# A gated cross-attention and ternary feed-forward block on one core: 16-bit tiles turned on TensorE in place of the DMA, one ring of eight PSUM banks, and new orders

## The chip, the core and the metric

The kernel runs on one core of one Trainium2 chip. The core has a matrix engine (TensorE, PE in the profile, with its weight loads shown apart as PEld), VectorE (DVE), ScalarE (ACT), GpSimd (POOL), and SyncE (SP), which here only issues DMAs. On-chip data lie in SBUF, 128 partitions wide; TensorE's results go to PSUM, which is used here as eight banks of 128 x 512 32-bit numbers. The metric is the device time of one execution in microseconds.

## The reference, cut to what matters

The input is 8 sequences of 512 tokens with 512 features, and for each sequence 64 context tokens. A first half adds a scaled cross-attention, a second half a scaled feed-forward block:

```python
def bit_linear(x, w, b):
    gamma_x = jnp.clip(jnp.max(jnp.abs(x), axis=-1, keepdims=True), 1e-05, None)
    scale_x = 127.0 / gamma_x
    x_dq = jnp.clip(jnp.round(x * scale_x), -128.0, 127.0) / scale_x
    ...
    gamma_w = jnp.clip(jnp.mean(jnp.abs(w)), 1e-05, None)
    w_dq = jnp.clip(jnp.round(w / gamma_w), -1.0, 1.0) * gamma_w
    ...
    return jnp.einsum('bsd,hd->bsh', x_ste, w_ste) + b
gate = jax.nn.silu(bit_linear(x, gate_w, gate_b))
val = bit_linear(x, val_w, val_b)
return bit_linear(gate * val, out_w, out_b)
...
x = x + jnp.tanh(g_xattn[0]) * _L0_xattn_ref(_layernorm(x, axis=-1), ctx_2048, mask_BxS2_ik0, ...)
x = x + jnp.tanh(g_ffn[0]) * _L0_ffn_ref(_layernorm(x, axis=-1), L0_ffn_gate_w, ...)
```

The attention has 16 heads of 32 features, masked softmax over the 64 context tokens, an output projection and a layernorm of its result. In the feed-forward block the activations are rounded to whole numbers from -128 to 127 per token and the weights to -1, 0 or 1; the hidden width is 2,048.

## The kernel before

A batch is one sequence, four token tiles of 128. Everything runs once, with the batches in a software pipeline: while the feed-forward tiles of batch b-1 are worked off, the attention of batch b and the layernorm of batch b+1 go on beside them. The stages that the change and the prediction touch are these, with their lines in the kernel before.

Layernorm and queries. Statistics come from VectorE and GpSimd (`ln1_stats`). For batches 0 and 1 the normalised tiles are turned by 32-bit transposes on TensorE (`ln1_turn`, L293). For the later ones the transposed input is loaded from memory (`load_turned`); the four means and four reciprocal deviations of each token are written to memory and read back spread over all partitions (`ln1_rows`, L228 and L230), so that a row of them holds, for each token in turn, eight numbers. VectorE subtracts the mean rows (L253), reading every eighth number, and GpSimd multiplies in two halves (L262). Queries are 4 x 4 32-bit matmuls (L304).

Attention. Scores (L340) of one half of the heads fill four banks, ScalarE takes the exponential (L353), TensorE sums (L367) and weighs the values (L415). The reciprocal sums travel over memory in four small DMAs (`rows`, `dense`, `over`, `R`). The projection (L442) is 4 x 4 32-bit matmuls for each token tile.

Feed-forward. For a token tile: `ffn_in` rounds on ScalarE and VectorE to whole numbers in 16 bits (`xq`), and a DMA transpose on SP's queue turns them (`xqT`, L687). `ffn_mid` fills four banks in each of two halves: four bias matmuls of 32 rows (L700), then 16 matmuls with the ternary gate and value weights (L705). `ffn_gate` takes silu on ScalarE (L715) and the product on VectorE (L716). `ffn_quant` finds the largest magnitude over 2,048 numbers (L734), `ffn_quant2` rounds a half on ScalarE (L752) and VectorE (L753) and again a DMA transpose turns it (`hqT`, L758). `ffn_out` is 16 matmuls (L766), `ffn_end` adds and stores. The scales of four tiles' tokens are turned by one DMA transpose for each batch (`uT`, L676).

PSUM. One pool of four banks (`bank`) serves all but the feed-forward's fours, which have a pool of four of their own (`psum4`, `four`). In the closing part every other four takes its banks from the first pool.

Order. `beginning`, `opening`, `attend_third`, `attend`, `attend_last` and `closing_flat` are lists written out by hand, one call after the other; `tile_in`, `tile_mid` and the like take the next token tile in their own sequence. `in_order` fixes each engine to the order in which its instructions were issued. So an instruction that waits holds up all behind it on its engine, and a DMA that waits holds up all behind it on SP's queue.

A second path, `general_path`, is there for inputs outside a common range. It isn't run with these inputs.

Of the kernel before, what the change touches and what calls it, by code (L numbers as in the profile page):

```python
# [9 lines left out]
F32 = mybir.dt.float32  # L10
# [7 lines left out]
P = 128  # L18
# [9 lines left out]
def common_path(  # L28
# [67 lines left out]
    psum = ctx.enter_context(tc.tile_pool(name="psum", bufs=4, space=bass.MemoryType.PSUM))  # L96
    psum4 = ctx.enter_context(tc.tile_pool(name="psum4", bufs=4, space=bass.MemoryType.PSUM))
# [5 lines left out]

    def bcast(vec, dst):
        nc.sync.dma_start(out=dst, in_=vec.partition_broadcast(P))

    ident = const.tile([P, P], F32, name="ident")
    make_identity(nc, ident)
    ones = const.tile([P, P], F32, name="ones")
    nc.gpsimd.memset(ones, 1.0)  # L110

    idle = psum4.tile([P, NW], F32, tag="four", name="idle")
# [110 lines left out]
    def ln1_rows(b):  # L223

        if b >= B:
            return
        rows = dram.tile([P, 2 * ST], F32, tag="lnrows", name="lnrows")
        nc.sync.dma_start(out=rows, in_=st_[b, "ln1"][1].rearrange("p r t -> p (r t)"))  # L228
        row = work.tile([P, P * 2 * ST], F32, tag="hs", name="row")
        nc.sync.dma_start(  # L230
            out=row, in_=rows.rearrange("p k -> (p k)").partition_broadcast(P)
        )
        row = row.rearrange("q (p r t) -> q r t p", r=2, t=ST)
        for i in range(2):
            st_[b, "row", i] = row[:, i].unsqueeze(1)
# [11 lines left out]
    def ln1_turned(b):  # L247

        if b >= B:
            return  # L250
        hT = st_[b, "hT"].rearrange("q c (t p) -> q c t p", t=ST)
        m = st_[b, "row", 0].to_broadcast([P, DC, ST, P])
        nc.vector.tensor_tensor(hT, hT, m, ALU.subtract)  # L253

    def ln1_turned_end(b):
        if b >= B:
            return
        hT = st_[b, "hT"].rearrange("q c (t p) -> q c t p", t=ST)
        r = st_[b, "row", 1].to_broadcast([P, DC // 2, ST, P])
        for h in range(2):  # L260
            half = hT[:, h * DC // 2 : (h + 1) * DC // 2]
            nc.gpsimd.tensor_tensor(half, half, r, ALU.mult)  # L262
# [250 lines left out]
    def ternary_load(name, *parts):  # L513

        w, chunks = {"gate": (gate_w, DC), "val": (val_w, DC), "out": (out_w, FC)}[name]
        if name not in st_:
            acc = [
                stage.tile([P, 1], F32, tag=f"acc{q}", name="acc", bufs=2) for q in range(DC)
            ]
            half = stage.tile([P, 3], F32, tag="half", name="half", bufs=2)  # L520
            st_[name] = {}, half, acc
# [9 lines left out]
    def magnitude(name, q, vector=False):  # L531
        part, _, acc = st_[name]
        if vector:
            nc.vector.tensor_reduce(
                acc[q], part[q], AX.X, ALU.add, apply_absolute_value=True
# [4 lines left out]
            junk, part[q], AF.Abs, accum_out=acc[q], saturate=False  # L540
        )

    def mean(i, name):
# [3 lines left out]
        for q in range(DC):  # L547
            nc.tensor.matmul(ps[:, 0:1], ones, acc[q], start=(q == 0), stop=(q == DC - 1))
        g = gw[:, i : i + 1]
        nc.vector.tensor_scalar(g, ps[:, 0:1], 1.0 / (F * D), 1e-5, ALU.mult, ALU.max)  # L550
# [71 lines left out]
    def ffn_stats(b, step):  # L622
# [47 lines left out]
        for r in range(4):  # L670
# [3 lines left out]
            )  # L674
        uT = fp.tile([P, ST, P], BF16, tag="uT", name="uT", bufs=2)
        nc.sync.dma_start_transpose(out=uT, in_=u.rearrange("p g k -> p (g k)"))  # L676
        st_[b, "in"] = rstd, sgv, uT

    def ffn_in(b, i):
# [4 lines left out]
        xq = fp.tile([P, D], BF16, tag="xq", name="xq", bufs=2)  # L684
        nc.vector.tensor_scalar(xq, h2, MAGIC, None, ALU.subtract)
        xqT = fp.tile([P, DC, P], BF16, tag="xqT", name="xqT", bufs=2)
        nc.sync.dma_start_transpose(out=xqT, in_=xq)  # L687
        st_[b, "xqT", i] = xqT
        st_[b, "h", i] = None

    def ffn_mid(b, i, jj, pool=psum4, tag="four"):


        xqT, uT = st_[b, "xqT", i], st_[b, "in"][2]
# [52 lines left out]
    def ffn_quant2(b, i, half):  # L747
        h, s = st_[b, "h", i], st_[b, "h_s", i]
        for half in (half,):
            cols = slice(half * F // 2, (half + 1) * F // 2)  # L750
            hq = fp.tile([P, F // 2], BF16, tag="hq", name="hq", bufs=2)
            nc.scalar.activation(h[:, cols], h[:, cols], AF.Identity, scale=s, bias=magic)  # L752
            nc.vector.tensor_scalar(hq, h[:, cols], MAGIC, None, ALU.subtract)  # L753

            late = b * ST + i - (B - 2) * ST
            pool, tag, bufs = (fp, "hqT", 2) if late < 0 else (xpool, f"x{late // 2 % 2}", ST)
            hqT = pool.tile([P, FC // 2, P], BF16, tag=tag, name="hqT", bufs=bufs)
            nc.sync.dma_start_transpose(out=hqT, in_=hq)  # L758
            st_[b, "hqT", i, half] = hqT
# [74 lines left out]
    def beginning():  # L834

        ternary_load("gate", 2)
        ternary_load("gate", 0)
        ternary_load("gate", 1)
        ternary_load("gate", 3)
        load_queries()  # L840
        load_x(ST, ST + 1)
        constants()
        ln1_stats(0, 0, 1)
        load_rows()
        later_rows()
        keys(0)
        keys(1)
        ternary_load("val", 0)
        keys(2)
        ln1_stats(0, 2, 3)  # L850
        keys(3)
        keys_end(0)
        ln1(0, 1)
        load_x(ST + 2, ST + 3)
        keys_end(1)
        context_values(0)
        ln1(0, 0)
        keys_end(2)
        keys_end(3)
        ln1_turn(0, 0)  # L860
        ln1_turn(0, 1)
        ln1(0, 2)
        context_values_end(0)
        ln1(0, 3)
        magnitude("gate", 0, True)
# [1161 lines left out]
```

## Time and profile before

The median of three runs is 724.24 us (722.26 to 726.79).

| | us |
|---|---|
| median of the runs | 724.24 |
| profiled execution, its own time | 719.48 |
| its span, first to last instruction | 717.6 |
| TensorE busy in it | 687.8 |
| VectorE busy | 559.0 |
| ScalarE busy | 361.5 |
| GpSimd busy | 175.5 |
| a steady batch (from 345.3 to 428.3) | 83.0 |

A row of a group gives the line of the kernel, engine and operation, output<-inputs, sizes and count; after the first bar the busy time of the group and the mean of one in ns; after the second the idle time of the engine just ahead of them, and what ended it. Bars of matmuls overlap, so the busy time of a group is less than count times mean. 32-bit matmuls of 512 columns leave two records each. A row of waits gives who waited for whom, the total in us, how often, and the longest. In the timeline the first number is the start, the second the length.

The other rows that matter for the change: the 64 DMA transposes of `hq` land 3.2 us after their issue and the 32 of `xq` 2.4 us after; the matmuls of 512 columns on 16-bit tiles have bars of 380 ns; a ScalarE copy of 128 x 512 out of PSUM (L377) takes 589 ns and a cast of 128 x 1024 (L615) 1,050 ns; the subtraction at L253 takes 3,872 ns and a multiplication at L262 2,901 ns.

### The profile page before, as it was taken

The numbers are of one execution on the slowest core, as the hardware profiler recorded it, in microseconds if no ns is written. First come the engines' busy times: TensorE is split into PE (matmuls) and PEld (weight loads), VectorE is DVE, ScalarE is ACT, GpSimd is POOL, SyncE is SP. The second block draws the span as 40 slices with busy tenths as digits, with TensorE's granted clock in tenths as the row PEclk, the third lists the DMA queues.
The fourth block names the chain that finished last, engine by engine and source line by source line (L and its number), as shares of the span: only waits on it lengthen the run. The fifth ranks groups of instructions, "written<-read, shape, count | busy, mean of one in ns | idle before, by whom it ended". The sixth has DMA issues, their size and how long they took to land.

```text
span 717.6 us, 9196 instructions
## 1 busy us (share of the span) xinstructions
PE 687.8 (96%) x3216; PEld 282.7 (39%) x3216; DVE 559.0 (78%) x961; ACT 361.5 (50%) x453; POOL 175.5 (24%) x207
## 2 busy tenths in 40 slices
PE   9999999989999999999999999999999899999996
PEld 5444333324443333433434333433434343443442
DVE  2578799989687895868968688678958748899783
ACT  1568728555336656238452563436552462355651
POOL 0153232326201064011631046010630120113000
PEclk9999999999999999999999999999999999999999
DMA  8977813153333444143422445135231233243434
GB/s 278 403 281 191 254 54 90 24 149 86 79 74 69 138 116 104 37 127 90 112 61 67 128 103 112 26 82 141 61 89 39 53 77 66 52 93 77 67 82 108
DMA packets 119432, 77.81 MB, mean 108 GB/s; under 512 B 98832, under 2 KB 98832, under 8 KB 118352
## 3 DMA queue, kind: packets, MB, share of 16 engines
q1 hardware_dynamic: 117264, 72.94, 38.7%
q10 hardware_dynamic: 2112, 4.19, 1.7%
q8 instruction: 27, 0.44, 0.3%
q14 instruction: 29, 0.24, 0.1%
HBM read 46.15 MB, written 8.94 MB: 77 GB/s over the span
## 4 chain that ended last, share of the span: by engine, by line
PE 68%; DVE 14%; DMA 7%; ACT 4%; POOL 3%; issue 2%; SPq 1%; DVEq 0%; ACTq 0%; POOLq 0%
PE four L705 23%; PE bank L766 11%; PE bank L442 11%; PE bank L304 8%; PE bank L705 3%; POOL hT L262 2%; DVE hT L253 2%; PE bank L340 2%; PE four L700 2%; DMA xqT<-xq 2%; PE bank L789 2%; DMA R<-over 2%; PE bank L803 1%; PE bank L367 1%; DMA rows<-den 1%
## 5 line engine op out<-in xcount | busy, mean ns | idle before, releaser
L705 PEld LDWEIGHTS <-xqT 128*128 128x128 bf16 x1024 | 94.9, 98 | 123.2 <-issue 14.0
L715 ACT ACTIVATE gate<-four,sgv 128x512 f32<-128x512 f32 x112 | 75.2, 686 | 104.8 <-PE four L705 103.5
L716 DVE SCALAR_TENSOR_TENSOR h<-four,sgv,gate 128x512 f32<-128x512 f32 x112 | 80.2, 742 | 60.7 <-PE four L705 30.0
L766 PE MATMUL bank<-out_tern,hqT 128*128 128x512 fp8e4 x512 | 116.8, 382 | 7.8 <-ACT prob L353 4.3
L442 PE MATMUL bank<-wo_sb,cT 128*128 128x512 f32 x256 | 115.4, 602 | 4.2 <-ACT prob L353 3.4
L304 PE MATMUL bank<-hT,wq_sb 128*128 128x512 f32 x256 | 115.7, 599 | 3.1 <-POOL hT L262 1.6
L705 PE MATMUL four<-gate_tern,xqT 128*128 128x512 fp8e4 x448 | 115.6, 380 | 2.0 <-DMA xqT<-xq 2.0
L705 PE MATMUL four<-val_tern,xqT 128*128 128x512 fp8e4 x448 | 115.0, 379 | 0.0
L752 ACT ACTIVATE h<-h,magic,h_s 128x1024 f32<-128x1024 f32 x64 | 76.1, 1235 | 74.4 <-DVE h_s L741 74.4
L766 PEld LDWEIGHTS <-hqT 128*128 128x128 bf16 x512 | 49.9, 98 | 75.9 <-issue 18.0
L743 POOL TENSOR_TENSOR so<-h_g,unit 128x1 f32<-128x1 f32 x32 | 8.5, 265 | 282.8 <-DVE h_g L739 282.8
L442 PEld LDWEIGHTS bank<-wo_sb,cT 128*128 128x128 f32 x256 | 48.2, 192 | 67.5 <-issue 53.0
L304 PEld LDWEIGHTS bank<-hT,wq_sb 128*128 128x128 f32 x256 | 47.3, 190 | 65.8 <-issue 53.9
L734 DVE TENSOR_REDUCE h_g<-h 128x1 f32<-128x2048 f32 (+1 forms) x32 | 71.8, 2245 | 0.6
L753 DVE TENSOR_SCALAR hq<-h 128x1024 bf16<-128x1024 f32 x64 | 56.5, 897 | 12.0 <-ACT h L752 11.7
L262 POOL TENSOR_TENSOR hT<-hT,row 128x1024 f32<-128x1024 f32 x12 | 34.6, 2901 | 64.3 <-DVE hT L253 64.3
L268 POOL TENSOR_TENSOR x<-x,bet_bc 128x512 f32<-128x512 f32 x32 | 47.2, 1504 | 9.4 <-issue 8.7
L315 ACT ACTIVATE qT<-bank,bq_sb 128x512 f32<-128x512 f32 x32 | 22.0, 686 | 53.1 <-PE bank L304 53.1
L645 POOL TENSOR_TENSOR x<-x,ob_bc 128x512 f32<-128x512 f32 x32 | 42.4, 1357 | 17.3 <-ACT h L644 17.3
L200 POOL TENSOR_TENSOR ln_r<-ln_r,mhalf 128x4 f32<-128x4 f32 x16 | 17.6, 1102 | 81.4 <-DVE ln_r L199 52.7
L377 ACT COPY den<-bank 128x512 f32<-128x512 f32 x32 | 17.2, 589 | 37.9 <-PE bank L367 36.5
L353 ACT ACTIVATE prob<-bank,esh,esc 128x512 f32<-128x512 f32 x40 | 27.9, 776 | 15.4 <-PE bank L340 15.4
(142 smaller groups left out, 763.9 us busy)
## 6 DMA issues: line engine op xcount, KB each, us to landing
x<-in_x SPq DMA_DIRECT2D x32, 256.0 KB, 2.8
R<-over SPq DMA_DIRECT2D x64, 128.0 KB, 2.7
out_x<-o SPq DMA_DIRECT2D x32, 256.0 KB, 2.4
hT<-in_xT SPq DMA_DIRECT2D x24, 256.0 KB, 3.6
wraw<-in_gate_w SPq DMA_DIRECT2D x4, 1024.0 KB, 14.1
wraw<-in_val_w SPq DMA_DIRECT2D x4, 1024.0 KB
wraw<-in_out_w ACTq DMA_DIRECT2D x4, 1024.0 KB
row<-lnrows SPq DMA_DIRECT2D x6, 512.0 KB, 3.4
```

Source lines behind the costliest of these rows:

```text
L262: nc.gpsimd.tensor_tensor(half, half, r, ALU.mult)
L268: nc.gpsimd.tensor_tensor(src, src, bet_bc, ALU.add)
L304: nc.tensor.matmul(ps, wq_sb[:, c, o * P : (o + 1) * P], hT[:, c, :], start=(c == 0), stop=(c == DC - 1),)
L442: nc.tensor.matmul(ps, st_[b, "cT", c][:, t * P : (t + 1) * P], wo_sb[:, c, :], start=(c == 0), stop=(c == DC - 1),)
L645: nc.gpsimd.tensor_tensor(xs, xs, ob_bc, ALU.add)
L705: nc.tensor.matmul(ps, xqT[:, c, :], w[:, c, cols], start=False, stop=(c == DC - 1))
L715: nc.scalar.activation(gate, four[2 * k], AF.Silu, scale=sgv[:, 0, i : i + 1])
L716: nc.vector.scalar_tensor_tensor(h[:, cols], four[2 * k + 1], sgv[:, 1, i : i + 1], gate, ALU.mult, ALU.mult)
L734: nc.vector.tensor_reduce(gx, h if part is None else h[:, F // 2 :], AX.X, ALU.max, apply_absolute_value=True)
L752: nc.scalar.activation(h[:, cols], h[:, cols], AF.Identity, scale=s, bias=magic)
L753: nc.vector.tensor_scalar(hq, h[:, cols], MAGIC, None, ALU.subtract)
L766: nc.tensor.matmul(ps, hqT[:, c % (FC // 2), :], weights["out"][:, c, :], start=(c == 0), stop=(c == FC - 1),)
```

## The change

The DMA transposes of the feed-forward block are replaced by transposes on TensorE: `ffn_turn`, `ffn_turn2` and `scale_turn` turn 4, 8 and 4 blocks of 128 x 128 16-bit numbers into one PSUM bank, and ScalarE copies the bank to SBUF. They are placed in the orders on their own, as `tile_turn`, `tile_turn2` and `scale_turn`. The two pools of PSUM become one of eight banks, taken in turn by everything. `ln1_rows` now turns the eight numbers of a token on TensorE, and `ln1_rows_end` copies them and sends them over memory, so that the row lies contiguous; the subtraction and the multiplication are both on VectorE, in halves (`ln1_turned(b, h, i)`). The sum of the weights' magnitudes takes one matmul and a small reduction in place of four matmuls. All six orders are new.

```diff
-    psum = ctx.enter_context(tc.tile_pool(name="psum", bufs=4, space=bass.MemoryType.PSUM))
-    psum4 = ctx.enter_context(tc.tile_pool(name="psum4", bufs=4, space=bass.MemoryType.PSUM))
+    psum = ctx.enter_context(tc.tile_pool(name="psum", bufs=8, space=bass.MemoryType.PSUM))
...
+    def turned(dtype):
+
+        return bank() if dtype == F32 else psum.tile([P, 2 * NW], dtype, tag="bank", name="turned")
...
+    ident16 = const.tile([P, P], BF16, name="ident16")
+    nc.gpsimd.tensor_copy(ident16, ident)
...
-        rows = dram.tile([P, 2 * ST], F32, tag="lnrows", name="lnrows")
-        nc.sync.dma_start(out=rows, in_=st_[b, "ln1"][1].rearrange("p r t -> p (r t)"))
-        row = work.tile([P, P * 2 * ST], F32, tag="hs", name="row")
+        ps = st_[b, "rows"] = bank()
+        nc.tensor.transpose(
+            ps[: 2 * ST, 0:P], st_[b, "ln1"][1].rearrange("p r t -> p (r t)"), ident
+        )
+
+    def ln1_rows_end(b):
+
+        if b >= B:
+            return
+        row = work.tile([P, 2, S], F32, tag="hs", name="row")
+        few = row[: 2 * ST, 0, 0:P]
+        nc.scalar.copy(few, st_[b, "rows"][: 2 * ST, 0:P])
+        rows = dram.tile([2 * ST, P], F32, tag="lnrows", name="lnrows")
+        nc.sync.dma_start(out=rows, in_=few)
         nc.sync.dma_start(
-            out=row, in_=rows.rearrange("p k -> (p k)").partition_broadcast(P)
+            out=row.rearrange("q r n -> q (r n)"),
+            in_=rows.rearrange("k p -> (k p)").partition_broadcast(P),
         )
-        row = row.rearrange("q (p r t) -> q r t p", r=2, t=ST)
         for i in range(2):
-            st_[b, "row", i] = row[:, i].unsqueeze(1)
+            st_[b, "row", i] = row[:, i, :].unsqueeze(1)
...
-    def ln1_turned(b):
+    def ln1_turned(b, h, i):
 
         if b >= B:
             return
-        hT = st_[b, "hT"].rearrange("q c (t p) -> q c t p", t=ST)
-        m = st_[b, "row", 0].to_broadcast([P, DC, ST, P])
-        nc.vector.tensor_tensor(hT, hT, m, ALU.subtract)
-
-    def ln1_turned_end(b):
-        if b >= B:
-            return
-        hT = st_[b, "hT"].rearrange("q c (t p) -> q c t p", t=ST)
-        r = st_[b, "row", 1].to_broadcast([P, DC // 2, ST, P])
-        for h in range(2):
-            half = hT[:, h * DC // 2 : (h + 1) * DC // 2]
-            nc.gpsimd.tensor_tensor(half, half, r, ALU.mult)
+        half = st_[b, "hT"][:, h * DC // 2 : (h + 1) * DC // 2, :]
+        row = st_[b, "row", i].to_broadcast([P, DC // 2, S])
+        nc.vector.tensor_tensor(half, half, row, ALU.mult if i else ALU.subtract)
...
-        for q in range(DC):
-            nc.tensor.matmul(ps[:, 0:1], ones, acc[q], start=(q == 0), stop=(q == DC - 1))
+        nc.tensor.matmul(ps[:, 0:DC], ones, acc, start=True, stop=True)
         g = gw[:, i : i + 1]
-        nc.vector.tensor_scalar(g, ps[:, 0:1], 1.0 / (F * D), 1e-5, ALU.mult, ALU.max)
+        nc.vector.tensor_reduce(g, ps[:, 0:DC], AX.X, ALU.add)
+        nc.vector.tensor_scalar(g, g, 1.0 / (F * D), 1e-5, ALU.mult, ALU.max)
...
+        st_[b, "in"] = rstd, sgv
+
+    def scale_turn(b):
+
+        ps = turned(BF16)
+        for i in range(ST):
+            nc.tensor.transpose(ps[:, i * P : (i + 1) * P], u[:, i, :], ident16)
         uT = fp.tile([P, ST, P], BF16, tag="uT", name="uT", bufs=2)
-        nc.sync.dma_start_transpose(out=uT, in_=u.rearrange("p g k -> p (g k)"))
-        st_[b, "in"] = rstd, sgv, uT
+        nc.scalar.copy(uT.rearrange("p t k -> p (t k)"), ps[:, : ST * P])
+        st_[b, "uT"] = uT
...
-        xq = fp.tile([P, D], BF16, tag="xq", name="xq", bufs=2)
+        xq = st_[b, "xq", i] = fp.tile([P, D], BF16, tag="xq", name="xq", bufs=2)
         nc.vector.tensor_scalar(xq, h2, MAGIC, None, ALU.subtract)
-        xqT = fp.tile([P, DC, P], BF16, tag="xqT", name="xqT", bufs=2)
-        nc.sync.dma_start_transpose(out=xqT, in_=xq)
-        st_[b, "xqT", i] = xqT
-        st_[b, "h", i] = None
-
-    def ffn_mid(b, i, jj, pool=psum4, tag="four"):
-
-
-        xqT, uT = st_[b, "xqT", i], st_[b, "in"][2]
+
+    def ffn_turn(b, i):
+
+        ps = turned(BF16)
+        for c in range(DC):
+            nc.tensor.transpose(
+                ps[:, c * P : (c + 1) * P], st_[b, "xq", i][:, c * P : (c + 1) * P], ident16
+            )
+        xqT = st_[b, "xqT", i] = fp.tile([P, DC, P], BF16, tag="xqT", name="xqT", bufs=2)
+        nc.scalar.copy(xqT.rearrange("p c t -> p (c t)"), ps[:, :D])
+
+    def ffn_mid(b, i, jj, pool=psum, tag="bank"):
+
+
+        xqT, uT = st_[b, "xqT", i], st_[b, "uT"]
...
-        for half in (half,):
-            cols = slice(half * F // 2, (half + 1) * F // 2)
-            hq = fp.tile([P, F // 2], BF16, tag="hq", name="hq", bufs=2)
-            nc.scalar.activation(h[:, cols], h[:, cols], AF.Identity, scale=s, bias=magic)
-            nc.vector.tensor_scalar(hq, h[:, cols], MAGIC, None, ALU.subtract)
-
-            late = b * ST + i - (B - 2) * ST
-            pool, tag, bufs = (fp, "hqT", 2) if late < 0 else (xpool, f"x{late // 2 % 2}", ST)
-            hqT = pool.tile([P, FC // 2, P], BF16, tag=tag, name="hqT", bufs=bufs)
-            nc.sync.dma_start_transpose(out=hqT, in_=hq)
-            st_[b, "hqT", i, half] = hqT
+        cols = slice(half * F // 2, (half + 1) * F // 2)
+        hq = st_[b, "hq", i, half] = fp.tile([P, F // 2], BF16, tag="hq", name="hq", bufs=2)
+        nc.scalar.activation(h[:, cols], h[:, cols], AF.Identity, scale=s, bias=magic)
+        nc.vector.tensor_scalar(hq, h[:, cols], MAGIC, None, ALU.subtract)
+
+    def ffn_turn2(b, i, half):
+
+        ps = turned(BF16)
+        for c in range(FC // 2):
+            nc.tensor.transpose(
+                ps[:, c * P : (c + 1) * P],
+                st_[b, "hq", i, half][:, c * P : (c + 1) * P], ident16,
+            )
+
+        late = b * ST + i - (B - 2) * ST
+        pool, tag, bufs = (fp, "hqT", 2) if late < 0 else (xpool, f"x{late // 2 % 2}", ST)
+        hqT = pool.tile([P, FC // 2, P], BF16, tag=tag, name="hqT", bufs=bufs)
+        st_[b, "hqT", i, half] = hqT
+        nc.scalar.copy(hqT.rearrange("p c t -> p (c t)"), ps)
...
     tiles = [(f, i) for f in range(B) for i in range(ST)]
-    done = dict.fromkeys(("in", "mid", "gate", "max", "quant", "out", "end"), 0)
+    done = dict.fromkeys(("in", "turn", "turn2", "mid", "gate", "max", "quant", "out", "end"), 0)
```

The new order of a steady batch:

```python
    def attend(b):
        tile_mid()
        sums(b, 0)
        tile_in()
        queries(b, 2)
        add_scaled(b - 1, 0, 1)
        tile_gate()
        sums_end(b, 0)
        spread(b, 0)
        queries(b, 3)
        tile_turn()
        tile_mid()
        queries_end(b, 2)
        add_scaled(b - 1, 2, 3)
        spread_end(b, 0)
        ln1_rows(b + 1)
        queries_end(b, 3)
        load_turned(b + 1)
        tile_mid()
        tile_gate()
        tile_max()
        scores(b, 1, psum, "bank")
        ln1_rows_end(b + 1)
        load_x((b + 2) * ST + 1)
        tile_gate()
        values(b, 0)
        values_end(b, 0)
        tile_quant()
        ffn_stats(b - 1, 0)
        tile_quant()
        tile_out()
        scores_end(b, 1)
        ffn_stats(b - 1, 1)
        tile_in()
        ln1_turned(b + 1, 0, 0)
        tile_turn2()
        tile_end()
        ln1_turned(b + 1, 1, 0)
        ln1_turned(b + 1, 0, 1)
        tile_mid()
        tile_turn2()
        tile_turn()
        ln1_turned(b + 1, 1, 1)
        tile_out()
        sums(b, 1)
        tile_gate()
        sums_end(b, 1)
        tile_max()
        tile_mid()
        spread(b, 1)
        tile_end()
        load_x((b + 2) * ST)
        queries(b + 1, 0)
        queries(b + 1, 1)
        spread_end(b, 1)
        ffn_stats(b - 1, 2)
        ffn_stats(b - 1, 3)
        tile_quant()
        tile_gate()
        tile_quant()
        queries_end(b + 1, 1)
        ffn_stats(b - 1, 4)
        tile_turn2()
        tile_turn2()
        tile_mid()
        tile_out()
        ffn_stats(b - 1, 5)
        tile_gate()
        add_beta(b + 1, *range(ST))
        tile_max()
        tile_in()
        queries_end(b + 1, 0)
        tile_end()
        tile_quant()
        values(b, 1)
        tile_quant()
        tile_turn()
        ln1_stats(b + 2, 0)
        scale_turn(b - 1)
        tile_turn2()
        load_x((b + 2) * ST + 2)
        values_end(b, 1)
        load_x((b + 2) * ST + 3)
        project_out(b, 0)
        tile_in()
        tile_mid()
        tile_gate()
        project_end(b, 0)
        tile_turn2()
        scores(b + 1, 0, psum, "bank")
        ln1_stats(b + 2, 1)
        scores_end(b + 1, 0)
        project_out(b, 1)
        tile_turn()
        tile_mid()
        project_end(b, 1)
        tile_gate()
        tile_out()
        project_out(b, 2)
        ln1_stats(b + 2, 2)
        tile_max()
        project_end(b, 2)
        tile_quant()
        pair_up(b + 1)
        tile_quant()
        tile_end()
        project_out(b, 3)
        tile_turn2()
        ln1_stats(b + 2, 3)
        check_sums(b)
        project_end(b, 3)
        tile_turn2()
        delta_scale(b)
```

In `beginning` and `opening` the same calls stand in other places; the calls of `attend_third`, `attend_last` and `closing_flat` are ordered anew as well, with the turns set in.

## The prediction

> **What bounds the kernel now.** I read the profile from the top: span and busy time of each engine, the chain that ended last, the costliest groups, then the waits of TensorE, then its instructions in order of time.
>
> ```profile
> span 717.6 us, 9196 instructions
> PE 687.8 (96%) x3216; PEld 282.7 (39%) x3216; DVE 559.0 (78%) x961; ACT 361.5 (50%) x453; POOL 175.5 (24%) x207
> PE 68%; DVE 14%; DMA 7%; ACT 4%; POOL 3%; issue 2%; SPq 1%; DVEq 0%; ACTq 0%; POOLq 0%
> L766 PE MATMUL bank<-out_tern,hqT 128*128 128x512 fp8e4 x512 | 116.8, 382 | 7.8 <-ACT prob L353 4.3
> L705 PE MATMUL four<-gate_tern,xqT 128*128 128x512 fp8e4 x448 | 115.6, 380 | 2.0 <-DMA xqT<-xq 2.0
> ```
>
> TensorE is busy 96% of the span and holds 68% of the chain. The groups that read the DMA-turned tiles waited only 2.0 us for `xqT`. The waits of TensorE:
>
> ```profile
> PE bank L766 <- ACT prob L353: 4.3, 5, 0.9
> PE bank L442 <- ACT prob L353: 3.4, 4, 0.9
> PE bank L766 <- DMA R<-over: 2.2, 1, 2.2
> PE four L705 <- DMA xqT<-xq: 2.0, 5, 0.8
> ```
>
> The steady batch (windows view; PE, PEld, DVE, ACT, POOL) shows the same: 80.7 of 83.0 us, at the full granted clock, with VectorE next at 66.0.
>
> ```profile
> 345.30:428.30 83.00, 80.69 (x384) 32.42 (x384) 65.96 (x112) 40.56 (x53) 22.94 (x27) 1.00 0.37 92
> ```
>
> A bar of TensorE is not its cost: a matmul's bar is 380 ns, but the next starts sooner. The timeline gives the steps:
>
> ```profile
> 22.95 1.04 PE L293 MATMUL bank<-ident,hs 128*128 128x128 f32 x8
> 23.83 3.60 PE L803 MATMUL bank<-wo_sb,cT_in 128*128 128x512 f32 x8
> 27.26 1.04 PE L293 MATMUL bank<-ident,hs 128*128 128x128 f32 x8
> ...
> 363.24 2.10 PE L340 MATMUL bank<-qT,kT 32*64 32x512 f32 x16
> 366.20 7.13 PE L442 MATMUL bank<-wo_sb,cT 128*128 128x512 f32 x16 [0.85 <-ACT prob L353]
> ```
>
> Eight f32 transposes go from 22.95 to 23.83, 110 ns each; eight f32 records of 512 columns from 23.83 to 27.26, 429 ns each. The chain's three last output groups give 10.40/48 = 217 ns for a 16-bit 512-column matmul. By these steps all of TensorE's work is: 1,536 x 0.216 = 331.8 (gate, value, output); 576 f32 records x 0.429 = 247.1; scores, sums and values 768 x 0.064 (1.02 us per 16) = 49; bias rows 256 x 0.081 = 21; small rest 9. That is 658 us. So 60 us of the span is not work: about 1.5 at the start, about 6 behind the last matmul, and some 52 of waits, of which the page shows only part as idle, since the tails of bars cover the rest. Gains have to come out of these 52.
>
> **The change, part by part.**
>
> *Transposes on TensorE.* 32 tiles x 4 (`ffn_turn`), 64 halves x 8 (`ffn_turn2`), 8 batches x 4 (`scale_turn`): 672 16-bit transposes of 128x128, plus 6 f32 ones for the layernorm rows. The nearest row is the f32 transpose, 110 ns, which is 429/4 and 3 ns more: it follows the columns. A 16-bit one is then 217/4 = 54 at least. The weight load is the other end: its 16-bit bar is 98 ns. But the f32 load's bar is 192 and it comes every 114 ns (7 in 0.80 us) when nothing holds it; the same ratio gives 98 x 0.6 = 58. I take 58: 672 x 0.058 = **39.0 us** (36 to 66 at 54 and 98). It lies on the path: TensorE sets the pace of every steady batch (84 of them there, 4.9 us on 83). The 6 f32 ones: 0.7 us.
>
> Here the Trainium skill speaks against the change more loudly than the trace: "TensorE: Matmul & The Clock Gate", section "Part 4: PE-mode transpose", puts such a transpose at about 275 ns in a kernel and says that the clock gate doesn't count it as busy. 672 x 0.275 would be 185 us and a time near 905. The bar agrees (273 ns median here), but the step is 110, so 275 is a latency and not what a queue of them costs; and the matmuls after the transposes at 23.83 keep 429 ns. I keep the row.
>
> *What the removed DMAs give.* 104 DMA transposes leave the SP queue (each holds it about 1.2 us, and lands 2.4 to 3.2 us later). What TensorE waited for them is 2.0 us. The rest was hidden behind matmuls. A lighter queue should also take the single 2.2 us wait for `R`. I count -2.2 for `R`; the 2.0 turn into the wait below.
>
> *New waits.* TensorE now waits twice in order: for the quantised tile, then for ScalarE's copy. In the new order the turn of `xq` stands directly ahead of a gate/value group 16 times. There the copy (nearest row: the 128x512 PSUM copy at L377, 589 ns) and the matmul's tail (0.16) stand against the four bias matmuls (0.33): 0.45 x 16 = **+7.2**; zero if one more group covered it, about 1 us each if ScalarE is late. The gate/value group behind it is queued, and so VectorE's and ScalarE's gating. The other 88 turns have an output group's first half (1.7 us), a gate/value group or a projection behind them, which hides the copy (128x1024: the cast at L615, 1.05 us). For waits on `hq` itself (ScalarE 1.19, VectorE 0.90 ahead of it) I count 0.05 each, **+4**; 0 to 0.25 each (0 to 22) as bounds.
>
> *ScalarE and VectorE.* Copies: 40 x 0.59 + 64 x 1.05 = 91 us, and ScalarE goes from 361 to about 452, 60% of the new span; per steady batch 40.6 + 11.4 = 52 of 88. No cost while TensorE leads; a late copy is priced above. The layernorm subtraction was 6 x 3.87 = 23.2 on VectorE; it becomes 24 halves, and the multiplication comes from GpSimd (12 x 2.90 = 34.6 leave it). A half on VectorE is 1.94 by its own strided row (3.87/2) and 1.36 by two 128x512 additions (L453, 0.68). At 1.36 that is 33, VectorE +10, 569 of 760: hidden under TensorE. The chain from rows to `hT` becomes some 4 us shorter (9.6 to 5.5), but TensorE waited for `hT` only 1.6 in all, so I count nothing.
>
> *The ring of eight banks.* At 363.24 the scores' 16 records are 1.02 us of steps, and the projection starts 2.96 later, since it needs a bank whose exponential isn't done; the other scores of a batch lose about 1.06 (325.22 to 327.30). About 3.0 a batch, 24 in all, is the most a deeper ring can give. Against it: gate/value groups have no banks of their own now, and in the new order the exponentials of the second scores come behind two quantisations (2.4) and an output group, with a gate/value group soon wanting those banks. Net between -24 and +10; I take **-6**.
>
> *The rest.* The mean's 4 matmuls become 1, three times: -1. The new orders move instructions without adding any; their gain is bounded by the 52 us of waits and is in the terms above. The opening (the first 135 us) has 128.7 busy, so at most 6 there: I count 0, +-4.
>
> Sum: 39.0 + 0.7 - 2.2 + 7.2 + 4 - 6 - 1 = **+41.7**. The profiled execution took 719.48 (span and 1.9 around it), so 761.2; the median of the runs is 724.24, 4.8 above it: 766, rounded to **765**.
>
> **The rivals.**
>
> A (the forecast), 750 to 780: transposes cost their steps, waits about even out. 70%.
>
> B, in-order waits pile up: TensorE stands at the 104 turns for quantisation or copy, because VectorE (80% of a batch) and ScalarE are late. At 0.25 us a turn, 26 in place of 11, and the ring giving nothing: 765 + 15 + 6 = 786. For it: the DMA path let TensorE run on while ScalarE waited 74 us for the scale at L752. Against: turns are mostly a group or more ahead of their use. 16%.
>
> C, the ring recovers all of its 24: 765 - 18 = 747. For it: the two waits on `prob` are the largest of TensorE's. 10%.
>
> D, not slower: the waits close as far as the transposes fill. The place is TensorE's 52 us of waits; it decides when they fall to 13. With the ring's full 24, the opening's 6, the 2.2, turns without waits and 54 ns a transpose: 724 + 36 - 24 - 6 - 2 - 1 = 727, just there. Each would have to come out at its best. 4%.
>
> **How the numbers follow.** The range takes C's lower part and B's upper part, 741 to 792. Within 1% (about what a measurement of this kernel can tell from no change) falls most of D: faster 0.01, same 0.03, slower 0.96.
>
> **What would show it.** In the profile after: a span near 759; transposes with starts about 58 ns apart inside a group; TensorE still about 95% busy, with some 39 us more steps; its waits for `prob` gone or smaller, and new ones for the ScalarE copies of `xqT`, 0.4 to 0.5 each at some 16 places; ScalarE near 450 busy; a steady batch of 87 to 89 us. Wrong if transposes step at 100 ns (about 793), if waits for `hq` or `hqT` exceed 20 us (B), or if the gaps behind the scores vanish (C).

## The result and the profile after

The changed kernel takes 766.56 us (766.15 to 768.63, four runs) against 724.75 before: a ratio of 1.058 (1.054 to 1.062). The forecast was 765, slower.

The page of the changed kernel: span, busy times, the chain by engine, and the groups that answer to those shown of before, with the new transposes (L776) and the copies (L785).

```profile
span 764.2 us, 10376 instructions
PE 726.6 (95%) x3876; PEld 321.5 (42%) x3876; DVE 539.3 (71%) x982; ACT 442.2 (58%) x563; POOL 137.2 (18%) x196
PE 81%; DVE 9%; ACT 4%; DMA 2%; issue 1%; SPq 0%; POOL 0%; DVEq 0%; POOLq 0%; ACTq 0%
L723 PE MATMUL bank<-gate_tern,xqT 128*128 128x512 fp8e4 x512 | 133.8, 384 | 1.7 <-ACT xqT L707 1.7
L792 PE MATMUL bank<-out_tern,hqT 128*128 128x512 fp8e4 x512 | 115.8, 379 | 1.1 <-ACT hqT L785 1.1
L785 ACT COPY hqT<-turned 128x1024 bf16<-128x1024 bf16 x64 | 63.7, 1015 | 75.3 <-PE turned L776 75.2
L776 PE MATMUL turned<-ident,hq 128*128 128x128 bf16 x512 | 38.3, 224 | 15.1 <-DVE hq L770 15.0
```

TensorE's busy time grew by 38.8 us, about the 39 that 672 transposes of 58 ns make; some 4 of it are matmuls at a lower clock (723.0 in a run below without such stretches). It leads still more than before: 81% of the chain in place of 68. The waits of TensorE show what took the place of the old ones:

```profile
PE turned L776 <- DVE hq L770: 15.0, 8, 4.8
PE bank L449 <- DVE cT L433: 4.5, 5, 3.0
...
PE bank L374 <- ACT prob L360: 0.9, 1, 0.9
```

The waits for the exponentials (`prob`), 8.6 us before in three rows (4.3, 3.4 and 0.9), are 0.9 now. In their place stand 15.0 us for `hq`, the tile that is still being rounded when its transposes are next in TensorE's queue. And a steady batch (windows view: the stretch and its length, then the busy time of PE, PEld, DVE, ACT and POOL with their instructions, the granted clock, the DMA share and GB/s):

```profile
349.40:434.70 85.30, 84.42 (x470) 37.11 (x470) 61.52 (x114) 50.47 (x67) 15.99 (x23) 1.00 0.19 60
```

85.3 us in place of 83.0, with TensorE waiting less than 1. The transposes inside it, in the timeline of TensorE:

```profile
373.00 1.06 PE L776 MATMUL turned<-ident,hq 128*128 128x128 bf16 x16
373.99 0.39 PE L718 MATMUL bank<-brow,uT 32*128 32x512 bf16 x4
...
383.57 0.62 PE L776 MATMUL turned<-ident,hq 128*128 128x128 bf16 x8 [0.60 <-DVE hq L770]
384.03 0.65 PE L449 MATMUL bank<-wo_sb,cT 128*128 128x512 f32 x1
```

Eight take 0.46 us from the first start to the next instruction: 58 ns each. Sixteen take 0.99: 62 each. The bar is 224 ns on average, but it isn't the cost.

### The profile page after: what moved, and what is told of

The parts are those of the page before. It is cut to its first block, busy times and chain, and to the rows that moved or that the text cites. A ratio compares the mean times of both kernels' runs of the same rounds, so it can differ in the third digit from the quotient of the medians.

```text
span 764.2 us, 10376 instructions
## 1 busy us (share of the span) xinstructions
PE 726.6 (95%) x3876; PEld 321.5 (42%) x3876; DVE 539.3 (71%) x982; ACT 442.2 (58%) x563; POOL 137.2 (18%) x196
## 4 chain that ended last, share of the span: by engine, by line
PE 81%; DVE 9%; ACT 4%; DMA 2%; issue 1%; SPq 0%; POOL 0%; DVEq 0%; POOLq 0%; ACTq 0%
PE bank L723 29%; PE bank L449 12%; PE bank L792 12%; PE bank L311 11%; PE turned L776 4%; PE bank L718 3%; PE bank L374 2%; PE bank L347 2%; PE bank L815 2%; PE bank L829 2%; ACT h L769 2%; DVE h_g L752 2%; DVE acc L539 1%; DVE hq L770 1%; PE bank L422 1%
## 5 line engine op out<-in xcount | busy, mean ns | idle before, releaser
L734 DVE SCALAR_TENSOR_TENSOR h<-bank,sgv,gate 128x512 f32<-128x512 f32 x128 | 92.2, 746 | 73.5 <-PE bank L723 36.7
L723 PE MATMUL bank<-gate_tern,xqT 128*128 128x512 fp8e4 x512 | 133.8, 384 | 1.7 <-ACT xqT L707 1.7
L723 PE MATMUL bank<-val_tern,xqT 128*128 128x512 fp8e4 x512 | 132.1, 380 | 0.0
L449 PE MATMUL bank<-wo_sb,cT 128*128 128x512 f32 x256 | 118.0, 606 | 4.5 <-DVE cT L433 4.5
L733 ACT ACTIVATE gate<-bank,sgv 128x512 f32<-128x512 f32 x128 | 85.3, 689 | 56.8 <-PE bank L723 52.7
L785 ACT COPY hqT<-turned 128x1024 bf16<-128x1024 bf16 x64 | 63.7, 1015 | 75.3 <-PE turned L776 75.2
L770 DVE TENSOR_SCALAR hq<-h 128x1024 bf16<-128x1024 f32 x64 | 45.2, 713 | 29.6 <-ACT h L769 29.6
L776 PE MATMUL turned<-ident,hq 128*128 128x128 bf16 x512 | 38.3, 224 | 15.1 <-DVE hq L770 15.0
L776 PEld LDWEIGHTS <-hq 128*128 128x128 bf16 x512 | 33.0, 100 | 33.9 <-DVE hq L770 21.5
L707 ACT COPY xqT<-turned 128x512 bf16<-128x512 bf16 x32 | 18.8, 588 | 45.3 <-PE turned L703 45.3
```

Of the source, the lines that this page charges most:

```text
L449: nc.tensor.matmul(ps, st_[b, "cT", c][:, t * P : (t + 1) * P], wo_sb[:, c, :], start=(c == 0), stop=(c == DC - 1),)
L723: nc.tensor.matmul(ps, xqT[:, c, :], w[:, c, cols], start=False, stop=(c == DC - 1))
L733: nc.scalar.activation(gate, four[2 * k], AF.Silu, scale=sgv[:, 0, i : i + 1])
L734: nc.vector.scalar_tensor_tensor(h[:, cols], four[2 * k + 1], sgv[:, 1, i : i + 1], gate, ALU.mult, ALU.mult)
L776: nc.tensor.transpose(ps[:, c * P : (c + 1) * P], st_[b, "hq", i, half][:, c * P : (c + 1) * P], ident16,)
L785: nc.scalar.copy(hqT.rearrange("p c t -> p (c t)"), ps)
```

## Experiments

The runs fall into five groups, each on one chip with the kernel before beside it, whose median lay between 724.5 and 726.8 us from group to group. Each ratio is against the kernel before of the same group. The changed kernel was run in the first group alone, so a difference from its 766.56 us is good to some 2 us; taken by the ratios instead, the differences below come out within 2 us of those given.

### The parts alone

**One ring of eight banks**, the rest as before:

```diff
-    psum = ctx.enter_context(tc.tile_pool(name="psum", bufs=4, space=bass.MemoryType.PSUM))
-    psum4 = ctx.enter_context(tc.tile_pool(name="psum4", bufs=4, space=bass.MemoryType.PSUM))
+    psum = ctx.enter_context(tc.tile_pool(name="psum", bufs=8, space=bass.MemoryType.PSUM))
...
-    def ffn_mid(b, i, jj, pool=psum4, tag="four"):
+    def ffn_mid(b, i, jj, pool=psum, tag="bank"):
...
```

and likewise for the scores in the opening, which took their banks from the second pool.

> The kernel before with one ring of eight PSUM banks in place of the two pools of four; nothing else is changed. Theory 1 (the transposes cost about 46 us of TensorE's path, and the change gives some 18 us of it back by the ring, since TensorE's excess behind the scores falls from 21 to 8 us between the two profiles): 725 - 18 = 707, with the waits of TensorE for the exponentials gone. Theory 2 (it is the new order of the calls that takes those waits away, and the ring alone only moves them, since the gate/value fours lose banks of their own): 720 to 730.

Measured: 724.14 us, ratio 1.0015 (0.998 to 1.005). Theory 1 falls: alone, the ring gives nothing, as theory 2 said. TensorE's waits with it:

```profile
PE bank L441 <- DVE cT L425: 10.3, 3, 9.3
...
PE bank L303 <- POOL hT L261: 4.0, 7, 0.9
PE bank L441 <- ACT prob L352: 3.4, 4, 0.9
```

Of the waits for `prob` 3.7 are left of 8.6 (3.4 here and 0.3 at the scores). But the wait for `hT` has grown from 1.6 to 4.0, and a steady batch, from one bias group to the same of the next batch, is still 83.0 us (412.9 to 495.9). The 9.3 us are in the opening, where the small DMAs behind `cT` landed late. That place differs between profiles of kernels that are alike there (1.9 us with ring and rows below, 7.5 and 8.3 in the last two kernels), so nothing is drawn from it.

**The layernorm rows alone**:

```diff
-        nc.sync.dma_start(out=rows, in_=st_[b, "ln1"][1].rearrange("p r t -> p (r t)"))
+        nc.tensor.transpose(
+            ps[: 2 * ST, 0:P], st_[b, "ln1"][1].rearrange("p r t -> p (r t)"), ident
+        )
...
-            nc.gpsimd.tensor_tensor(half, half, r, ALU.mult)
+        nc.vector.tensor_tensor(half, half, row, ALU.mult if i else ALU.subtract)
```

> The kernel before with the layernorm rows of the change alone: eight numbers turned on TensorE, contiguous rows, both operations on VectorE in four halves, at the places where the old calls stood. Theory 1: TensorE waited 1.6 us for hT, and VectorE's busy time falls a little (contiguous halves near 1.2 us): 722 to 727. Theory 2 (the multiplication now loads the engine that is second to TensorE, and the wait for the small transpose and copy holds TensorE and ScalarE at once): 730 or more.

Measured: 717.94 us, ratio 0.992 (0.989 to 0.994), 6 us less than before in the medians. Both theories missed it, the second by its sign. A contiguous half takes 1,218 ns, so four take 4.9 in place of 3.9 and two GpSimd halves of 2.9 behind it; no wait for the `hT` of the later batches is left among TensorE's, and a steady batch takes 82.4 us (403.0 to 485.4). That accounts for half: the spans of the two profiled executions differ by 3.0 us (717.6 and 714.6), 2.8 of it in the four steady batches. The other half lies in how the runs spread (716.0 to 723.4, against 718.0 to 729.0) and is not explained.

**Ring and rows together**, in the order of before (the two edits above).

> The kernel before with the ring of eight banks and the contiguous layernorm rows together, its own order and its DMA transposes. Theory 3 (in a steady batch the waits for the exponentials that the ring removes are paid back as waits for hT, since the chain of layernorm rows is as long as the batch; contiguous rows shorten that chain, so only both together gain): a steady batch of 80 to 81 us in place of 83 and 82.4, 705 to 712 in all. Rival (the batch is bound by something else, TensorE's steps with the waits of the order): 716 to 720, as with the rows alone.

Measured: 716.89 us, ratio 0.988 (0.984 to 0.993), a steady batch of 83.0 (402.0 to 485.0). Theory 3 falls: with the wait for `hT` gone the ring still gives no more than the rows alone. In this order TensorE waited 8.3 us for `hqT` from the DMA and 3.4 for `prob`.

### What the transposes cost

**Back on the DMA**, in the new order:

```diff
     def ffn_quant2(b, i, half):
...
         nc.vector.tensor_scalar(hq, h[:, cols], MAGIC, None, ALU.subtract)
...
+        nc.sync.dma_start_transpose(out=hqT, in_=hq)
...
     def ffn_turn2(b, i, half):
-
-        ps = turned(BF16)
...
-        nc.scalar.copy(hqT.rearrange("p c t -> p (c t)"), ps)
+        pass
```

and likewise for `xq` and `u`.

> The kernel after, with its ring, rows and orders, but with the 104 transposes back on the DMA (issued from SP behind each quantisation); the turns on TensorE and ScalarE's copies are left out. Theory 1 (steps of 672 transposes and their group ends, some 47 us, and 15 us of waits for hq ahead of them, are what the change costs): 766.6 - 47 - 12 = 708, below the kernel before. Theory 2 (the new orders themselves are what is slower, and the transposes partly fill waits): 735 to 755.

Measured: 775.65 us, ratio 1.071 (1.065 to 1.077). Slower than with TensorE's transposes, outside both theories. The waits and the clock say why:

```profile
PE bank L776 <- DMA hqT<-hq: 28.1, 10, 5.9
PE bank L449 <- DVE cT L433: 15.3, 8, 4.9
PE bank L714 <- DMA xqT<-xq: 11.9, 3, 4.0
```

The granted clock over the span is 0.968, against 0.987 in the changed kernel: an estimate from that (span times what is missing from 1) gives 25 us lost in place of 10. The new orders leave little between a rounding and the use of the turned tile. The old ones leave enough for a DMA. So the order belongs to the transposes, and this run doesn't price either.

**Twice**:

```diff
         for c in range(FC // 2):
-            nc.tensor.transpose(
+            for _ in range(2):
+                nc.tensor.transpose(
...
```

> The kernel after with each of the 672 sixteen-bit transposes issued twice into the same place. Theory 1 (a transpose is a step of 58 ns on the path): 766.6 + 39 = 806, 800 to 808 if some of them fall into waits. Rival (a transpose costs its latency, some 220 ns, or the clock falls while transposes run): above 840. Rival (they fill waits and are nearly free): below 780.

Measured: 797.31 us, 30.8 more than the changed kernel: 46 ns for each added transpose. It lies between theory 1 (806) and the cheap rival (below 780), and far below the dear one (above 840). TensorE's busy time rose by 36.8 us (763.4 from 726.6), so the steps are there; about a fifth of them fell into waits that were there anyway. The price is even: 15.6 us for 336 transposes in four batches, from the first value matmuls of the fourth batch to those of the last, and 10.2 for 220 in the closing part behind them, 46 ns each in both.

**Left out, with the copies kept**:

```diff
     def ffn_turn2(b, i, half):
...
-        nc.scalar.copy(hqT.rearrange("p c t -> p (c t)"), ps)
+        nc.scalar.copy(hqT.rearrange("p c t -> p (c t)"), st_[b, "hq", i, half])
```

> The kernel after without its 672 sixteen-bit transposes: ScalarE copies the quantised tile as it lies, SBUF to SBUF, at the same place of the order, so the tiles are left unturned and the matmuls compute with them as they are; everything else, the waits for hq included, stays. Theory 1 (steps of 58 ns and some 0.08 us at each of 104 group ends lie wholly on the path): 766.6 - 47 = 719 to 722. Rival (a part of them fills waits, as the second set of transposes added 31 and not 39): 730 to 736.

Measured: 720.22 us, 46.3 less than the changed kernel, as theory 1 said, though not for its reason, as the next section shows. A steady batch in the windows view, and the waits that lead:

```profile
324.70:406.70 82.00, 79.94 (x386) 31.97 (x385) 62.09 (x114) 50.85 (x66) 16.21 (x23) 1.00 0.20 60
```

```profile
PE bank L449 <- DVE cT L433: 9.7, 6, 2.2
PE bank L777 <- ACT hqT L770: 4.8, 4, 1.7
```

A batch is 82.0 to 82.2 long, so its 84 transposes cost 3.1 to 3.3 us of 85.3, less than their 4.9 of steps: part of them fills the waits for `cT` and `hqT` that show here. All waits for `hq` at TensorE are gone, since without transposes TensorE goes on with the next group while ScalarE waits.

### The waits for hq

In the third batch the changed kernel waits twice for long. The timeline of TensorE at the first place, and the windows view of the 7 us behind that wait and behind the second one (granted clock in the third column from the end):

```profile
156.36 1.04 PE L776 MATMUL turned<-ident,hq 128*128 128x128 bf16 x8 [4.37 <-DVE hq L770]
157.33 0.61 PE L718 MATMUL bank<-brow,uT 32*128 32x512 bf16 x4
157.88 1.89 PE L723 MATMUL bank<-gate_tern,xqT 128*128 128x512 fp8e4 x4
159.56 1.65 PE L723 MATMUL bank<-val_tern,xqT 128*128 128x512 fp8e4 x4
161.04 1.03 PE L723 MATMUL bank<-gate_tern,xqT 128*128 128x512 fp8e4 x4
```

```profile
156.30:163.40 7.10, 7.04 (x37) 3.34 (x38) 2.92 (x6) 3.53 (x4) 0.00 (x0) 0.68 0.43 140
...
238.30:246.50 8.20, 8.10 (x53) 3.66 (x54) 4.16 (x7) 5.76 (x7) 1.12 (x1) 0.73 0.00 0
```

After 4.4 us without work the transposes step at 121 ns and the first gate matmuls at 420, twice their usual; from 161 on they are at 217 again. The granted clock of that stretch is 0.68, which costs 7.1 x 0.32 = 2.3 us more, and 8.2 x 0.27 = 2.2 at the second place. The Trainium skill has a rule for this in "TensorE: Matmul & The Clock Gate", section "HAM oscillation — how this bites in real kernels": a gap of more than some 3.4 us drops the clock to half. The trace agrees: behind waits of 4.4 and 4.8 us the steps are about twice as long.

So the turns at the two places were moved behind the next gate/value group, and at the first place the scaled addition on VectorE behind both roundings:

```diff
     def attend_third():
...
-        add_scaled(b - 1, 0, 1)
         load_turned(b + 1)
         tile_quant()
         values(b, 0)
-        tile_turn2()
         tile_quant()
+        add_scaled(b - 1, 0, 1)
         values_end(b, 0)
         tile_mid()
+        tile_turn2()
...
         tile_quant()
         tile_quant()
+        tile_mid()
+        sums(b + 1, 0)
         tile_turn2()
         tile_turn2()
```

The group and the sums moved here are taken out of the next batch's list.

> The kernel after with two of its turns moved behind the next gate/value group in the third batch's order, and the scaled addition moved behind the quantisation that it held up on VectorE. Theory 1 (two waits of 4.4 and 4.8 us for hq there, and some 2.3 us of halved clock behind each, are a part of the loss that belongs to the order and not to the transposes): 752 to 756. Rival (the waits move to what is next in the queue, since VectorE is late there anyway): 762 to 767.

Measured: 755.39 us, ratio 1.041 (1.038 to 1.044), 11.2 less than the changed kernel, and so theory 1. The waits for `hq` that are left:

```profile
PE turned L776 <- DVE hq L770: 6.2, 7, 1.5
```

The granted clock of its span is 0.997 in place of 0.987. So 11.2 of the 46.3 were these two waits with their slow clock, and 755.39 - 720.22 = 35.2 (both kernels in one group) is what the transposes cost without them: 52 ns each on average.

The 35.2 are not steps alone. They hold the 6.2 us of shorter waits for `hq`, and whatever the turned tiles cost by taking PSUM banks, since the kernel with the copies alone takes none for them; no run tells these apart. Nor is the price even. The same four batches took 12.9 us more than without transposes, 38 ns for each of 336. The closing part took 17.4 more for 220, or 79 ns each. The closing part without and with the transposes:

```profile
575.30:718.00 142.70, 133.88 (x659) 55.63 (x658) 106.77 (x193) 90.70 (x115) 17.02 (x28) 0.99 0.08 29
...
592.50:752.60 160.10, 147.64 (x879) 69.01 (x878) 107.66 (x193) 91.94 (x116) 16.74 (x28) 1.00 0.07 26
```

There TensorE's waits for quantised tiles and for ScalarE's copies and gates come to 6.6 us, against 3.2 without transposes.

### ScalarE's copies

```diff
         nc.scalar.copy(hqT.rearrange("p c t -> p (c t)"), ps)
+        nc.scalar.copy(hqT.rearrange("p c t -> p (c t)"), ps)
```

and likewise for `xqT` and `uT`.

> The kernel after with each of ScalarE's 104 copies of turned tiles issued twice (some 85 us more on ScalarE, 442 to 527 busy). Theory 1 (the copies are hidden under TensorE): 766 to 772. Rival (ScalarE's queue sets when the turned tiles, the gates and the exponentials come, so the copies are on the path): 780 or more.

Measured: 794.37 us, 27.8 more: the rival, by far. ScalarE is at 526.6 busy, still 66% of the span.

```profile
PE turned L778 <- DVE hq L772: 17.8, 10, 4.8
PE bank L795 <- ACT hqT L788: 6.8, 13, 1.7
...
PE bank L725 <- ACT xqT L709: 3.5, 3, 1.6
PE turned L704 <- DVE xq L698: 3.3, 5, 1.2
```

Many short waits, at the copies and at roundings that come later because ScalarE does. An engine with a third of its time free is on the path when others stand in order behind it. But a second copy, directly between a transpose and its use, is dearer than the first; so the first was taken away:

```diff
     def ffn_turn2(b, i, half):
...
+        st_[b, "hqT", i, half] = st_[b, "hq", i, half].rearrange("p (c t) -> p c t", t=P)
```

> The kernel after with the transposes and 96 of ScalarE's copies left out: the matmuls read the quantised tiles as they lie, from four buffers each, so they are unturned and computed with as they are; ScalarE still copies the eight tiles of scales, and the order is unchanged. Beside the run with the copies alone (720.2) it tells what the copies cost. Theory 1 (the copies as they are hide under TensorE, and only a second set of them, which comes ahead of the output group's matmuls, does not): 715 to 720. Rival (ScalarE is on the path already, as 28 us for the second set suggest): 700 to 708.

Measured: 714.12 us, 6.1 less than with the copies kept, a little below the range of theory 1 and far from the rival. It bounds from above what the copies cost beside no transposes, since the tiles have four buffers here in place of two and two; the two kernels lie in different groups, so it is good to some 2 us. What TensorE waits for a copy that stands between a transpose and its use is in the 35.2 above.

### The depth of the ring, and a better order

The kernel with the turns moved, with seven banks in place of eight (`bufs=7`).

> The kernel with the two turns moved (755.4), its ring of PSUM banks one bank shorter, seven in place of eight. Theory 5 (in the changed kernel, where turned tiles take banks of the ring too, its depth is what keeps TensorE from waiting for exponentials, copies and gates): 762 to 775. Rival (the order alone keeps the banks free in time and the eighth is slack): 754 to 758.

Measured: 771.09 us, 15.7 more: theory 5. The waits for `hq` stay (5.7 us), and the others of TensorE are spread over many rows of under 3 us, on copies, gates and sums, among them

```profile
PE turned L776 <- ACT hqT L785: 2.3, 2, 1.2
...
PE bank L718 <- ACT gate L733: 1.6, 6, 0.6
```

So one pool of eight was worth nothing in the old order, while in the new one, where the turned tiles take banks too, the eighth bank is worth 16 us. That it is the turned tiles that need it wasn't tested, and the new order with two pools of four wasn't tried.

Two steps to a better kernel started from ring and rows with the DMA transposes. The first moves the gate ahead of the next batch's scores:

```diff
+        tile_gate()
         scores(b + 1, 0, psum, "bank")
         project_out(b, 0)
         scores_end(b + 1, 0)
         ln1_stats(b + 2, 0)
-        tile_gate()
```

> The kernel before with ring, contiguous rows, and in the steady batch the gate moved ahead of the next batch's first scores. Theory 4 (with the ring, the projection behind the scores takes a bank that the gate frees, and the gate stands behind the exponentials on ScalarE, 2.1 us in each of the batches): 4 x 2 = 8 us less than with ring and rows, 708 to 711. Rival (the exponentials come later by the gate, and the next user of their banks waits instead): 715 to 719.

Measured: 715.74 us, ratio 0.987 (0.979 to 0.995). The steady batch fell to 81.7 us (406.9 to 488.6), 1.3 less than with ring and rows, where theory 4 said 2.1; in all the time lies where the rival put it and can't be told from ring and rows.

The second step also moves an output group in the third batch:

```diff
-        tile_out()
         sums(b, 1)
         ffn_stats(b - 1, 0)
-        tile_end()
         tile_max()
         tile_mid()
+        tile_out()
+        tile_end()
```

> As the kernel with the gate moved, and in the third batch the first output group behind the next gate/value group, since it waits there 5.2 us for the DMA transpose of hq and TensorE's clock falls behind it. Theory 4: another 5 to 7 us, 702 to 706. Rival (what is behind it waits for VectorE instead): no change against the kernel with the gate alone.

Measured: 718.72 us, ratio 0.991 (0.988 to 0.993): the rival. The wait for `hqT` there went, and the groups that followed started 2.9 and 2.8 us late in its place (2.5 of it for `xqT`). Rows alone (0.992), ring and rows (0.988) and the gate moved (0.987) are all about 1% faster than the kernel before; among them the runs don't decide.

## Why the prediction was right

The total was right to 2 us, and the direction for the reason given: the transposes' steps lie on TensorE's path, and little comes back for them. The terms came out less well, and that their errors cancel is luck.

| term | predicted | measured | from |
|---|---|---|---|
| transposes on TensorE | 39.7 | 35.2 | turns moved, less copies alone |
| waits around the turns | 7.2 + 4 | 11.2 | changed kernel, less turns moved |
| ScalarE's copies | 0 | up to 6.1 | copies alone, less no copies |
| ring, rows, mean, `R`, orders | -9.2 | -10.6 | no copies, less before |
| sum | +41.7 | +41.9 | |

The measured column adds up by itself, as a chain of differences; what it shows is the division.

*Transposes.* The step of 58 ns, scaled from the f32 row by the ratio of weight loads, is what the trace shows. What failed is that it lies on the path alike everywhere, with 4.9 us in each steady batch: there the 84 cost 3.1 to 3.3, in the closing part they cost more than their steps (79 ns), and the average is 52 (46 for a second set). At 275 ns each, the figure that the prediction set aside, the kernel would have come to 905; the bar is 224 and the step 58, so the row was the right choice.

*Where it fell.* A steady batch was to take 87 to 89 us and took 85.3, only 2.3 more than before. Four such batches make 9 of the 46.6 us by which the span grew. The closing part alone makes 19.4, 160.1 us in place of 140.7, with 220 transposes on top of the same 659 matmuls; before and after:

```profile
576.90:717.60 140.70, 132.96 (x659) 55.73 (x658) 108.77 (x193) 63.79 (x81) 17.91 (x28) 0.99 0.37 79
...
604.10:764.20 160.10, 147.67 (x879) 68.99 (x878) 107.64 (x193) 92.12 (x116) 16.71 (x28) 0.99 0.08 25
```

*New waits.* Equal in sum by chance; besides, 6.2 us of the waits for `hq` are in the table's row of the transposes. The 16 x 0.45 (its parts, 0.59 + 0.16 - 0.33, give 0.42) for copies ahead of gate/value groups was wrong: a turn there is mostly of the next token tile, while the group behind it is the second half of the tile before, so it waits for nothing. `xqT` cost 1.7 + 0.4 us. The waits for `hq`, priced at 0.05 each, came as 15.0 us, of which 9.2 at two places where the order puts the turn too early. There the bound (0 to 22) held and the value didn't. That such a wait also slows what follows, 2.2 us each, was missed.

*ScalarE.* "No cost while TensorE leads" was wrong in its reason: doubling the copies costs 28 us at 66% busy. For the one set that the kernel has, the error is at most some 6 us.

*The ring.* -6 was about what ring, rows and small parts gave together, but it was put to the wrong part. Alone the ring gave 0 and the rows gave -6 (-3 in the profiled spans), against 0 in the prediction, which took the 1.6 us of waits for `hT` as all that the rows could give. In the new order the eighth bank is worth 16 us; a price for it can't be read off the old order's waits.

*VectorE.* Predicted 569 busy, measured 539: a half of the rows takes 1.22 us and not 1.36 (3 us in all), the rounding of `hq` fell from 897 to 713 ns on average (11 us), and two small operations on `x_g` fell from 11.4 to 2.7 us together. The rest is spread over small groups.

*Rivals.* B's mechanism, TensorE standing in order for `hq`, was there, at two places rather than at 104. C's was there too: the waits for `prob` fell by 7.7 us, by ring and new order together. Rival D needed all waits down to 13 us. What the transposes had to pay against was not there: in the new order without any transposes or copies, the time is 714.

## What to carry to other kernels

In this kernel, with TensorE busy 96% of the span, work that moved onto it from a DMA was paid for in the main: 52 ns of a step of 58 on average, but 38 in the steady batches and 79 in the closing part. Against that stood the 2 us that TensorE had waited for those DMAs. Cost a short matmul by its distance to the next start, and an added engine step by who stands in order behind it, not by its busy share. Forecast stages as well as the total: here the total was right and the steady batch wasn't. A wait of over 4 us on TensorE is to be counted with the slow stretch behind it, 2.2 to 2.3 us here.

## What the runs showed of the hardware that was not expected

The rounding of `hq` on VectorE has a median of 694 ns in the kernel before, but up to 1,777 ns. Fourteen of the 64 take over 1.2 us, and each of these starts while GpSimd is in one of its large additions or multiplications. In the timeline of VectorE, and of GpSimd, before:

```profile
442.57 3.45 DVE L753 TENSOR_SCALAR hq<-h 128x1024 bf16<-128x1024 f32 x2 [0.58 <-ACT h L752]
```

```profile
441.29 5.86 POOL L268 TENSOR_TENSOR x<-x,bet_bc 128x512 f32<-128x512 f32 x4
```

Two roundings take 3.45 us while GpSimd adds. All fourteen end 0.55 us after the GpSimd instruction in which they started: the longest took 1,777 ns where 1,227 of that instruction were left, the shortest 1,236 where 687 were left. It looks as if the rounding stands until GpSimd is done. In the changed kernel the median is 688 and the mean 713; only two take over 1 us, 1,254 and 1,734 ns, with 704 and 1,185 left. That the one holds up the other is read from these times; no run tested it.

The kernel before lay between 718 and 729 us in the largest group, of 30 runs, and this spread is larger than some of the effects that the runs were after. The profiles of kernels with the same opening differ there by up to 7 us in the landing of small DMAs; that this is the cause of the spread wasn't tested.
